# A transformer block on one core: the first token chunks prepared ahead of a branch, and a feed-forward part in 2 KB pieces

## The chip, the cores and the metric

The kernel runs on one core of a Trainium2 chip. The core has a matrix engine (TensorE, PE in the profile, with its weight loads listed as PEld), a vector engine (VectorE, DVE), a scalar engine (ScalarE, ACT), a general engine (GpSimd, POOL), and SyncE (SP), which issues the transfers between HBM and on-chip memory here. Each engine works through its own queue of instructions in order and waits on semaphores for the others. On-chip memory is SBUF (128 partitions) and PSUM, where matmuls leave their results.

The metric is device time in microseconds (us) of one execution, the median of several runs. Lower is better.

## The reference, cut to what matters

Two sequences of 1,024 tokens with 512 features go through an attention part and a feed-forward part. Each part has a layer norm ahead of it and one behind it, and adds its input.

```python
def _layernorm(x, axis=-1, eps=1e-05):
    m = jnp.mean(x, axis=axis, keepdims=True)
    v = jnp.var(x, axis=axis, keepdims=True)
    return (x - m) / jnp.sqrt(v + eps)
# attention, 32 query heads, 8 key heads, head size 128
q, k, v = hidden @ Wq, hidden @ Wk, hidden @ Wv        # each key head serves 4 query heads
gs = log_sigmoid(k) / 16
o_lin = gla_scan(softmax(q), softmax(k), v, gs)        # S = S * exp(g) + k v^T;  o = q S
y = sliding_window_attn(rope(q), rope(k), v)           # window of 64
o = bfloat16(0.5 * y + 0.5 * o_lin) @ Wo
# feed-forward, 1376 hidden features, weights rounded to NF4 in blocks of 64
h = silu(x @ dq1.T) * (x @ dq2.T)
f = h @ dq3.T
# the block
x = x + _layernorm(attention(_layernorm(x)))
x = x + _layernorm(feed_forward(_layernorm(x)))
```

## The kernel before

The 2,048 tokens are 16 chunks of 128 (NCI). A chunk is loaded, normed on DVE (bn_stats, bn_aggr, an addition, then the power of −1/2 on POOL, called `rstd`, then one subtract-and-multiply; L143 to L157), and transposed by four PE transposes into `xnT`, which holds all tokens with the features across the partitions.

The program has four stages.

**Ahead of a branch (L1162 to L1180).** All of Wk is loaded in four quarters of 512 KB (`wka`). Each is squared on ACT, its columns are summed by matmuls with ones on PE (`norms`), and DVE takes the greatest sum and compares it (`small_gates`). The flag is read by every engine and picks the fast attention (taken here) or a general one.

**Start of the fast attention (from L262).** Chunks 0 to 3 are loaded, normed (`input_norms`) and transposed (`input_transposes`; tiles `xtp`). Then the weights of key head 0 are loaded (`load_weights`: `wkv`, `wq`, `wo`), then the tables of the rotary embedding (`fcos`, `fsin`) and four constants. `part_weights` splits Wo of one head into two parts on POOL, a cast and a subtraction per query head (tile `wop`), for all four heads ahead of the first chunk (L654). Then comes the first chunk, stage by stage: `key_products` (tile `pk`), `key_softmax`, `query_products` (`pq`), whose rotary embedding (`rope`) is four POOL instructions (`qtmp`, two halves `qr`, their sum `qr`), softmaxes, and three kinds of transposes (`pt`, `tr`, `tq`).

**The attention's loop (L670 to L751).** It runs over 128 steps n, one per key head g, sequence b and chunk c of 128 tokens. Each step's order is written out by hand: `scores` (`ps`), masks on DVE, decays, exponentials on ACT, the next chunk's `query_products`, the linear part (`pa`, `ot`), `mix`, `values`, the projection of the chunk before (`project`: eight matmuls into `py`) and its sum (`collect`: `yacc`), and the next state (`pS`, `S`). The engine handles of this part are `InOrder`: what is called through them keeps the program's order on its engine, and all such instructions show the helper's line, L116. Calls through plain `nc` handles, as the norms of tokens, may be moved by the scheduler.

Two more chunks of input are normed and transposed in each of the steps n = 0 to 5:

```python
inputs = list(range(2 * CB + 2 * n, min(2 * CB + 2 * n + 2, NCI)))   # CB = 2
```

The NF4 rounding of the feed-forward weights runs inside this loop in 544 small steps on DVE and ACT, six in an even step n and three in an odd one, with its first at `BEGIN` = 6. It loads rows of weights (`xw`) and writes the rounded ones to HBM (`dq`).

**The feed-forward part (`feed_forward`, L1067).** A block is 512 tokens; there are four. `tokens` (L1104) loads a chunk of x (`xc`), norms the attention's sum (`yn`), adds, norms again (`xn`), and transposes into `x2T` (tiles `tx`). `up_weights` and `down_weights` load rounded weights (`row`, `col`) and transpose them on PE (`tw`, `tw3`) into three big tiles `w1T`, `w2T`, `w3T`. For each of 11 slices f of the hidden features, PE computes `pgate` and `pup` (L1136), ACT a sigmoid, DVE two products into `hT`. Four output chunks follow (`pf`, L1154), each normed, added and stored. The weights of slice f+2 are prepared beside slice f of the first block; the tokens of the next block are prepared at the odd f from 1 to 7. All these calls go through plain handles. The tiles lie in pools that open where the attention's pools close.

Of the kernel before, what the change touches and what calls it, by code (L numbers as in the profile page):

```python
# [1 line left out]

# [9 lines left out]
F32 = mybir.dt.float32  # L12
BF16 = mybir.dt.bfloat16
F32R = mybir.dt.float32r
# [17 lines left out]
NFT = (FF + P - 1) // P  # L32
EPS = 1e-5
# [86 lines left out]
def sandwich_kernel(ctx: ExitStack, tc: tile.TileContext, x, wq, wk, wv, wo, w1, w2, w3, out, con):  # L120
# [17 lines left out]
    yacc = keep.tile([P, NCI, HID], F32)  # L138
    dq1 = dram.tile([FF, HID], F32)
# [3 lines left out]
    def norm_stats(src):  # L143

        st = small.tile([P, 6], F32)
        nc.vector.bn_stats(st, src)
        mv = small.tile([P, 2], F32)
        nc.vector.bn_aggr(mv, st)
        ve = small.tile([P, 1], F32)
        nc.vector.tensor_scalar(ve, mv[:, 1:2], EPS, None, ALU.add)  # L150
# [4 lines left out]
    def normed(dst, src):  # L155
        mean, rstd = norm_stats(src)
        nc.vector.tensor_scalar(dst, src, mean, rstd, ALU.subtract, ALU.mult)  # L157
# [91 lines left out]
    def transposed_inputs(xtp, work, ptr):  # L249
        xnT = xtp.tile([P, KT, T], F32)  # L250
        for ci in range(NCI):
            xc = work.tile([P, HID], F32, tag="s", name=f"x{ci}")
            nc.sync.dma_start(xc, x[ci * P : (ci + 1) * P, :])
            xn = work.tile([P, HID], F32, tag="a", name=f"xn{ci}")
            normed(xn, xc)
            tp = ptr.tile([P, KT, P], F32, tag="tr", name=f"xtp{ci}")
            for kt in range(KT):
                nc.tensor.transpose(tp[:, kt, :], xn[:, kt * P : (kt + 1) * P], ident)
            nc.scalar.copy(xnT[:, :, ci * P : (ci + 1) * P], tp)
        return xnT  # L260

    def fast_attention():  # L262

        with ExitStack() as attn:
            fc = attn.enter_context(tc.tile_pool(name="fc", bufs=1))
            fs = attn.enter_context(tc.tile_pool(name="fs", bufs=4))
            xtp = attn.enter_context(tc.tile_pool(name="fxtp", bufs=1))
            wp = attn.enter_context(tc.tile_pool(name="fwp", bufs=2))
# [17 lines left out]
            xnT = xtp.tile([P, KT, T], F32)  # L286

            tokens = {}

            def input_norms(ci):  # L290

                xc = qz.tile([P, 576], F32, tag="zx", name=f"x{ci}", bufs=2)[:, :HID]
                nc.sync.dma_start(xc, x[ci * P : (ci + 1) * P, :])
                xn = qz.tile([P, 576], F32, tag=("zp", "zm")[ci % 2], name=f"xn{ci}", bufs=(2, 1)[ci % 2])[:, :HID]
                normed(xn, xc)
                tokens[ci] = xn

            def input_transposes(ci):
                xn = tokens.pop(ci)
                tp = ptr.tile([P, KT, P], F32, tag="tr", name=f"xtp{ci}")  # L300
                for kt in range(KT):
                    transpose(tp[:, kt, :], xn[:, kt * P : (kt + 1) * P])
# [909 lines left out]
```

## Time and profile before

| | us |
|---|---|
| median of 3 runs | 2175.61 (2174.6 to 2177.53) |
| the profiled execution, its own time | 2172.86 |
| its span in the trace | 2171.1 |
| PE busy in the span | 2104.6 (97%) |
| DVE busy | 1489.6 (69%) |
| ACT busy | 1362.9 (63%) |
| POOL busy | 944.1 (43%) |

The profile shows one execution. PE is the engine with the most work, and the chain of waits that ended last lies on it for 90% of the span. An average over the whole span says little about the two ends, so the view to look for is a table of busy time by stretch, in which the stages stand side by side: ahead of the branch (to 16 us), start of the attention (to 39 us), the loop (to about 1,660), the hand-over (to 1,712) and the feed-forward part. An entry in a timeline gives start and length in us, engine, line, operation, the tiles written and read (out<-in), the shape, how many instructions were put together, and in brackets how long the engine had been idle and which instruction released it. The mean granted clock of PE over the span was 0.988 of full speed.

### The profile page before, as it was taken

What the parts mean: (1) busy time and instruction counts of PE and PEld (TensorE: products, weight loads), DVE (VectorE), ACT (ScalarE), POOL (GpSimd) and SP (SyncE); (2) the same over time, 40 slices, a digit from 0 to 9 for tenths busy, and PEclk for the clock granted to TensorE, in tenths of its full rate; (3) what the DMA queues carried; (4) which work ended last, traced back from release to release, by engine and by line L of the source; (5) the groups of instructions that cost most, each with busy time, mean ns of one, the idle gap of its engine ahead of it and who ended that gap; (6) DMA issues with size and microseconds to landing.
All of it is one profiled execution on the core that took longest, in us unless ns stands there. A gap on an engine that the chain in (4) does not pass through costs nothing.

```text
span 2171.1 us, 27563 instructions
## 1 busy us (share of the span) xinstructions
PE 2104.6 (97%) x8948; PEld 1409.9 (65%) x8948; DVE 1489.6 (69%) x2822; ACT 1362.9 (63%) x3944; POOL 944.1 (43%) x1290
## 2 busy tenths in 40 slices
PE   4999999999999999999999999999996999999998
PEld 2667777777777777777777777777774544444443
DVE  3668888888788888888888888888887425142222
ACT  2568888888888888888888888888884210101000
POOL 3445555655475556456555655565452101010000
PEclk7999999999999999999999999999998999999999
DMA  5100100010010001000100100000002301000000
GB/s 194 45 15 11 59 11 15 25 49 11 9 58 10 15 15 59 11 10 20 53 11 15 39 33 11 12 11 20 13 6 68 115 27 39 0 29 0 20 0 21
DMA packets 45192, 64.52 MB, mean 30 GB/s; under 512 B 3632, under 2 KB 19632, under 8 KB 45040
## 3 DMA queue, kind: packets, MB, share of 16 engines
q1 hardware_dynamic: 45040, 62.67, 8.8%
q8 instruction: 73, 1.20, 0.2%
q14 instruction: 79, 0.65, 0.1%
HBM read 50.01 MB, written 12.65 MB: 29 GB/s over the span
## 4 chain that ended last, share of the span: by engine, by line
PE 90%; POOL 3%; ACT 2%; DVE 2%; DMA 1%; issue 1%; POOLq 0%; ACTq 0%; SPq 0%; DVEq 0%
PE pq L116 19%; PE py L116 10%; PE pk L116 10%; PE ot L116 9%; PE pgate L1136 7%; PE pf L1154 7%; PE pup L1136 7%; PE pa L116 7%; PE ps L116 5%; PE tr L116 3%; PE tq L116 3%; PE pg L116 2%; POOL qr L116 1%; PE pS L116 1%; PE pt L116 1%; ACT ps L116 1%
## 5 line engine op out<-in xcount | busy, mean ns | idle before, releaser
L116 PE MATMUL pq<-wq,xnT 128*128 128x512 f32 x1024 | 460.6, 592 | 0.0
L116 POOL TENSOR_TENSOR qtmp<-q,fcos 128x512 f32<-128x512 f32 x128 | 162.0, 1266 | 580.3 <-ACT q L116 580.3
L116 PEld LDWEIGHTS pq<-wq,xnT 128*128 128x128 f32 x1024 | 184.9, 190 | 183.7 <-issue 183.6
L116 ACT ACTIVATE zs<-xw,fbounds 128x512 bf16<-128x512 f32 (+3 forms) x416 | 287.8, 723 | 0.0
L116 PE MATMUL py<-wop,oc 128*128 128x512 f32 x1024 | 270.5, 406 | 1.3 <-ACT oc L116 1.3
L152 POOL TENSOR_TENSOR rstd<-ve,mhalf 128x1 f32<-128x1 f32 x64 | 35.7, 565 | 515.0 <-DVE ve L150 499.0
L116 ACT ACTIVATE ps<-ps,nms 128x128 f32<-128x128 f32 x512 | 175.0, 342 | 110.7 <-DVE nms L116 94.7
L116 PE MATMUL pk<-wkv,xnT 128*128 128x256 f32 x1024 | 233.4, 381 | 0.0
L116 ACT ACTIVATE pq<-pq,nmq 128x128 f32<-128x128 f32 x512 | 175.1, 342 | 91.7 <-DVE nmq L116 79.2
L1139 ACT ACTIVATE sg<-pgate 128x512 f32<-128x512 f32 (+1 forms) x44 | 26.2, 597 | 324.9 <-PE pgate L1136 324.9
L116 PEld LDWEIGHTS pk<-wkv,xnT 128*128 128x128 f32 x1024 | 195.9, 191 | 47.0 <-issue 14.1
L116 PEld LDWEIGHTS py<-wop,oc 128*128 128x128 f32 x1024 | 182.9, 189 | 36.6 <-ACT oc L116 1.7
L116 POOL TENSOR_TENSOR qr<-q,fsin 128x256 f32<-128x256 f32 x256 | 206.0, 825 | 0.0
L116 DVE SCALAR_TENSOR_TENSOR zp<-zp,zs 128x512 f32<-128x512 f32 (+3 forms) x224 | 195.4, 872 | 9.4 <-ACT zs L116 5.0
L116 POOL TENSOR_TENSOR qr<-qr,qtmp 128x512 f32<-128x512 f32 x128 | 165.8, 1295 | 9.8
L116 DVE SCALAR_TENSOR_TENSOR zm<-zm,zs 128x512 f32<-128x512 f32 (+3 forms) x192 | 163.0, 849 | 5.7 <-ACT zs L116 3.0
L1136 PE MATMUL pgate<-x2T,w1T 128*128 128x512 f32 (+1 forms) x352 | 160.4, 594 | 0.0
L1136 PE MATMUL pup<-x2T,w2T 128*128 128x512 f32 (+1 forms) x352 | 158.2, 592 | 0.0
L116 DVE TENSOR_TENSOR ps<-ps,fwin 128x512 f32<-128x512 f32 x128 | 89.2, 697 | 96.3 <-PE ps L116 95.4
L1154 PE MATMUL pf<-w3T,hT 128*128 128x512 f32 (+1 forms) x352 | 151.8, 592 | 0.0
L116 PE MATMUL ps<-kT,qrT 128*128 128x128 f32 x1024 | 136.5, 276 | 0.2
L116 DVE TENSOR_REDUCE nmq<-pq 128x4 f32<-128x512 f32 x128 | 87.8, 686 | 59.4 <-ACT q L116 59.4
(125 smaller groups left out, 4078.9 us busy)
## 6 DMA issues: line engine op xcount, KB each, us to landing
wq<-in_L_attn_Wq_dram SPq DMA_DIRECT2D x8, 1024.0 KB, 6.1
wo<-in_L_attn_Wo_dram SPq DMA_DIRECT2D x8, 1024.0 KB, 5.1
xw<-in_L_ffn_w_dram SPq DMA_DIRECT2D x20, 256.0 KB, 2.6
dq<-zp SPq DMA_DIRECT2D x20, 256.0 KB, 2.0
row<-dq SPq DMA_DIRECT2D x20, 256.0 KB, 2.8
x<-_attn_hidden_states_dram SPq DMA_DIRECT2D x16, 256.0 KB, 2.7
xc<-_attn_hidden_states_dram SPq DMA_DIRECT2D x16, 256.0 KB, 2.6
out_dram<-res SPq DMA_DIRECT2D x16, 256.0 KB, 2.0
```

The lines of the kernel that those rows point to most:

```text
L116: return lambda *args, **kwargs: self.tc.keep_in_program_order(getattr(self.engine, name)(*args, **kwargs))
L152: nc.gpsimd.tensor_tensor(rstd, ve, mhalf, ALU.pow)
L1136: nc.tensor.matmul(pg[:n, :], lhsT=wT[:, kt, f * P : f * P + n], rhs=x2T[:, kt, :], start=kt == 0, stop=kt == KT - 1)
L1139: nc.scalar.activation(sg[:n, :], ps[0][:n, :], AF.Sigmoid)
L1154: nc.tensor.matmul(pf, lhsT=hT[:n, f, m * P : (m + 1) * P], rhs=w3T[:n, f, :], start=f == 0, stop=f == NFT - 1)
```

## The change

Five things change.

1. Ahead of the branch, chunks 0 to 3 are loaded between the quarters of Wk, then the first `wkv` and `wq` and both tables. The four chunks are normed in place and transposed there, in an order written out for DVE, ACT and PE. `xnT`, the weight tiles (two sets) and the tables are now permanent tiles.
2. Chunks 4 to 15 are loaded after the branch into eight places of a tile `tokens`, which takes the second buffer of `wop`; `wo` and the small constants come after x4 and x5. A chunk's place is loaded again (12 to 15) once it was transposed.
3. `part_weights` of key head 0 is called for two heads behind the first chunk's transposes and for two inside step n = 0.
4. Two chunks of input in the steps n = 0 and 1, then one per step to n = 9. `BEGIN` is 2.
5. The feed-forward part becomes a class: 44 separate pieces of 2 KB per partition (`w1`, `w2`, `w3`, `hT`, 11 each) in place of the big tiles; buffers of tokens, rows and columns in the attention's `wqs`, `wos` and `tables`; transposed tokens written over `xnT`; and all its calls on DVE, ACT and PE through `InOrder` handles, in this order for the first block: tokens and transposes of chunks 0 to 3, row transposes of slices 0 and 1 for both weights, then the loop. The matmuls and transposes are as many as before.

```diff
+    xnT = keep.tile([P, KT, T], F32)
+    wkvs = [keep.tile([P, KT, 2 * D], F32, name=f"wkv{i}") for i in range(2)]
+    wqs = [keep.tile([P, KT, GRP * D], F32, name=f"wq{i}") for i in range(2)]
+    wos = keep.tile([P, GRP, HID], F32)
+    tables = keep.tile([P, 2, NCH, D], F32)
...
+    def chunk_transposed(xn, ci, ptr, transpose, copy):
+        tp = ptr.tile([P, KT, P], F32, tag="tr", name=f"xtp{ci}")
+        for kt in range(KT):
+            transpose(tp[:, kt, :], xn[:, kt * P : (kt + 1) * P])
+        copy(xnT[:, :, ci * P : (ci + 1) * P], tp)
...
+            staging = parts_tile("tokens").rearrange("p i h d -> p (i h) d").bitcast(F32)
+            def staged(ci):
+                return staging[:, ci % (2 * GRP), :]
             def input_norms(ci):
...
+                normed(staged(ci), staged(ci))
             def input_transposes(ci):
...
+                chunk_transposed(staged(ci), ci, ptr, transpose, nc.scalar.copy)
+                if ci + 2 * GRP < NCI:
+                    chunk_loaded(staged(ci + 2 * GRP), ci + 2 * GRP)
...
-            for ci in range(2 * CB):
-                input_norms(ci)
-                input_transposes(ci)
-            weights = {0: load_weights(0)}
+            for ci in range(AHEAD, AHEAD + 2):
+                chunk_loaded(staged(ci), ci)
...
+            weights = {0: (*first_weights, parts_tile("wop0"), load_out_weights(0))}
             qb = load_const("fbounds", [P, 16], F32, con["bounds"])
+            for ci in range(AHEAD + 2, AHEAD + 2 * GRP):
+                chunk_loaded(staged(ci), ci)
...
-            for h in range(GRP):
-                part_weights(0, h)
             key_products(0)
...
             softmax_transposes(0)
-            BEGIN = (NCI - 2 * CB) // 2
+            for h in range(2):
+                part_weights(0, h)
+            arriving = iter(range(AHEAD, NCI))
+            BEGIN = 2
             for n in range(N_):
                 g, b, c = chunks[n]
-                inputs = list(range(2 * CB + 2 * n, min(2 * CB + 2 * n + 2, NCI)))
+                inputs = list(islice(arriving, 2 if n < 2 else 1))
...
                     for ci in inputs[1:]:
                         input_norms(ci)
+                    if n == 0:
+                        for h in range(2, GRP):
+                            part_weights(0, h)
...
+        def tokens(self, ci, xc):
+            yn = self.next("yn")
+            normed(yn, yacc[:, ci, :], self.vector)
+            self.vector.tensor_tensor(yacc[:, ci, :], xc, yn, ALU.add)
+        def token_norms(self, ci):
+            xn = self.next("xn")
+            normed(xn, yacc[:, ci, :], self.vector)
+            return xn
...
+        def hidden(self, f, gate, up, sg):
+            n = min(P, FF - f * P)
+            self.vector.tensor_tensor(sg[:n, :], sg[:n, :], gate[:n, :], ALU.mult)
+            self.vector.tensor_tensor(self.hT[f][:n, :], sg[:n, :], up[:n, :], ALU.mult)
+        def run(self, f0, ready):
...
+                for f in range(f0 if tb == 0 else 0, NFT):
+                    gate = self.up_product(0, tb, f)
+                    sg = self.sigmoid(f, gate)
+                    if row:
+                        self.up_weights(0, row[0], row[1][0])
+                    if tb == 0:
+                        col = next_down(col)
+                    up = self.up_product(1, tb, f)
+                    if row:
+                        self.up_weights(1, row[0], row[1][1])
+                        row = loaded_up(next(ups, None))
+                    self.hidden(f, gate, up, sg)
...
+                    ci = (tb + 1) * self.MB + (f - 2) // 2
+                    if f >= 2 and ci < min(NCI, (tb + 2) * self.MB):
+                        if f % 2 == 0:
+                            if xn is not None:
+                                self.token_transposes(ci - 1, xn)
+                            xc = self.load_tokens(ci)
+                        else:
+                            self.tokens(ci, xc)
+                            xn = self.token_norms(ci)
...
+            F.xc, F.yn, F.xn, F.sg = ([wqs[i][:, j, :] for i in range(2)] for j in range(4))
+            F.rows = [wos[:, j, :] for j in range(4)]
...
+            for ci in range(F.MB):
+                F.tokens(ci, F.load_tokens(ci))
+                F.token_transposes(ci, F.token_norms(ci))
             for f in range(2):
-                up_weights(f)
...
+                for i in range(2):
+                    F.up_weights(i, f, F.load_up(i, f))
+            F.run(0, 2)
...
         for kt in range(KT):
             nc.sync.dma_start(wka[:, kt, :], wk[kt * P : (kt + 1) * P, :])
-            nc.scalar.activation(wka[:, kt, :], wka[:, kt, :], AF.Square)
+            if kt % 2:
+                for ci in (kt - 1, kt):
+                    chunk_loaded(chunks[ci], ci)
+        first_weights = load_weights(0)
+        load_tables("fcos", "fsin")
...
+        for ci in range(2):
+            normed(chunks[ci], chunks[ci], vector)
+        squares(0)
+        squares(1)
+        transposed(0)
+        squares(2)
+        transposed(1)
+        squares(3)
+        normed(chunks[2], chunks[2], vector)
         most = wkp.tile([1, 2], F32)
-        nc.vector.tensor_reduce(most, norms, AX.X, ALU.max)
+        vector.tensor_reduce(most, norms, AX.X, ALU.max)
...
+        normed(chunks[3], chunks[3], vector)
+        transposed(2)
+        transposed(3)
```

## The prediction

> **What bounds the kernel now.** I read the table of busy time by stretch first (stretch; its length, busy time and instructions of PE, PEld, DVE, ACT, POOL; granted clock; share of the DMA engines; GB/s).
>
> ```profile
> 0.00:16.00 16.00, 8.70 (x16) 1.44 (x16) 1.50 (x3) 5.51 (x5) 0.77 (x8) 1.00 0.35 131
> 16.00:39.00 23.00, 3.61 (x15) 2.89 (x16) 8.24 (x17) 1.75 (x3) 10.20 (x14) 0.57 0.77 243
> 85.00:114.00 29.00, 27.49 (x137) 20.09 (x136) 18.11 (x45) 17.55 (x57) 13.40 (x22) 1.00 0.12 35
> 169.00:1642.00 1473.00, 1471.03 (x7000) 1082.12 (x6998) 1224.40 (x2275) 1213.06 (x3563) 841.45 (x1117) 1.00 0.07 23
> 1660.00:1680.00 20.00, 9.17 (x37) 6.00 (x35) 10.92 (x25) 2.42 (x8) 2.33 (x4) 0.78 0.49 157
> 1680.00:1712.00 32.00, 25.75 (x92) 14.96 (x93) 22.20 (x55) 9.29 (x15) 6.27 (x11) 0.82 0.43 132
> 1712.00:2125.00 413.00, 413.00 (x1065) 188.09 (x1064) 119.44 (x225) 38.80 (x67) 15.55 (x28) 1.00 0.07 21
> ```
>
> PE is full from 169 to 1642 us and from 1712 to 2125 us. Its idle time, 66 us, lies at both ends and where the attention hands over to the feed-forward part; only there can the change win or lose, since the matmul and transpose counts stay. Next, the timeline between the branch and the first key product (start, length, engine, line, instruction, idle before it):
>
> ```profile
> 29.36 0.61 POOL L116 CAST wop<-wo 128x512 fp32r<-128x512 f32 x1 [7.13 <-DMA wo<-in_L_attn_Wo_dram]
> 30.01 0.69 DVE L146 BATCH_NORM_STATS2 st<-x 128x6 f32<-128x512 f32 x1 [7.20 <-DMA x<-_attn_hidden_states_dram]
> ...
> 33.72 0.55 POOL L152 TENSOR_TENSOR rstd<-ve,mhalf 128x1 f32<-128x1 f32 x1
> 34.24 1.26 POOL L116 TENSOR_TENSOR wop<-wo,wop 128x512 fp32r<-128x512 f32 x1
> 34.31 1.48 DVE L157 TENSOR_SCALAR xn<-x,mv,rstd 128x512 f32<-128x512 f32 x1 [2.59 <-POOL rstd L152]
> ...
> 39.30 1.06 PE L116 MATMUL pk<-wkv,xnT 128*128 128x256 f32 x2
> ```
>
> Chunk 2's tokens arrive late, then its `rstd` (a power, on POOL) waits behind the casts and subtractions of part_weights, and pk of chunk 0 starts at 39.30. The reader should also see that an `xn` beside a POOL subtraction takes 1.48 us; the two at 21.65 took 1.16 together. Last, the hand-over:
>
> ```profile
> 1668.52 0.69 DVE L116 TENSOR_TENSOR yacc<-yacc,py 128x512 f32<-128x512 f32 x1 [3.64 <-PE py L116]
> 1671.14 0.69 DVE L1110 TENSOR_TENSOR yacc<-xc,yn 128x512 f32<-128x512 f32 x1 [1.48 <-DMA xc<-_attn_hidden_states_dram]
> 1678.23 0.55 DVE L157 TENSOR_SCALAR xn<-yacc,mv,rstd 128x512 f32<-128x512 f32 x1 [0.53 <-POOL rstd L152]
> 1682.44 0.55 DVE L157 TENSOR_SCALAR xn<-yacc,mv,rstd 128x512 f32<-128x512 f32 x1 [0.59 <-POOL rstd L152]
> 1690.90 1.49 PE L1136 MATMUL pgate<-x2T,w1T 128*128 128x512 f32 x2
> ```
>
> Four token chunks come at 4.2 us each, because the scheduler put the next chunk's statistics beside this one's.
>
> **Part 1, ahead of the branch.** Removed behind it: four x loads, their norms and sixteen transposes, the loads of the first weights and tables. Added before it: the same. Squares take 1.06 us each on ACT, the norms' matmuls of one quarter about 1.75 us (16 from 5.67 to 14.37, the first slow), a group of four transposes 1.1 with its copy .58. In the new hand-written order, PE does quarter 0 until 9.07, quarter 1 until 10.8, tx0 to 11.25, quarter 2 from 13.0 (its square waits behind copy 0 on ACT), tx1, quarter 3 until 18.72. Maximum and comparison take 1.57, so the flag stands at about 20.3 instead of 15.97: +4.3. The norm of chunk 3 and its transposes end at 23.9. After the flag the branch took .7 (SP) to 1.0 (POOL). In SP's queue the x loads stand between the quarters, and weights and tables behind them: the last square started at 8.26 with 2 MB read, 1 MB of x adds 2.5 us at the quarters' pace (.5 MB in 1.26), 2.5 MB of weights and tables 7.7 at the 341 GB/s that the hand-over reached: about 18.5, so the flag and not a load sets the start. The first pk then starts at about 24.5, instead of 39.30: −14.8, give or take 1 for the waits within the two interleaved chains.
>
> **Part 2, what that gain runs into.** part_weights moves from ahead of the first chunk into it: eight POOL instructions (casts of .61, subtractions of 1.26). In the compiled order of the new kernel a cast, a subtraction and a cast stand ahead of the rope of the first queries, a subtraction inside it, four more in n=0. In the old trace (S is the start of pk) the rope's last addition ended at S+14.17; now at S+17.35. Behind POOL's queue stand the `rstd` of chunks 6, 7, 8 and 11, and DVE, in its own order, waits for each before qs(0), the mask of scores(0) and qs(1). Followed instruction by instruction with the old durations: mask(0) S+24.25 instead of S+18.15, pa(0) S+27.0 instead of S+21.4, scores of n=1 S+39.6 instead of S+30.86. That is 8.75 lost of the 14.8; I add .5 for n=1. The first of them waits for wo, now issued at about 26 behind x4, x5 and three constants; with the median landing of 5.1 it is there at 31, ahead of its turn at 33.9 (S+9.4); with the 10.1 that the first wo took here, POOL waits 2.3 more. Bounds: nothing lost, if the part_weights lie in POOL's idle time (POOL is busy 9.85 of the 18 us after 39), and 14.8, all of it. I take the followed chain, as it uses the new order. Net −5.55.
>
> **Part 3, the loop.** Inputs come one per n for n=2 to 9, formerly two for n=0 to 5. Transposes stay 1.09 per chunk, but the second of each old pair waited .67 for the ACT copy of the first (2.0 us in three for the first 100 us), and its pairs' own seam goes too: .84 for each of four n, −3.4. Bounds −3.4 and 0. The rounding steps start at n=2 instead of 6, while DVE also has the norms. One full pair of n costs DVE 19.7 to 20.7 us of 25 with rounding (stretches of 25 us from 169 on); two input norms add 2×1.6 (.69+.18+.14+.55), against a PE pair of 24.9+2×1.1=27.1. DVE keeps 3 us spare: 0. If each `rstd` waits as long as the one above (2.59), that is eaten, which is rival C. At the end no rounding stands beside the last ropes: −.35 (the slowed ones on POOL there); bounds 0 and −1.
>
> The 1.48 us norm beside POOL lost .9 against .58 for its like; if all eight norms meet a POOL operation, DVE loses 7.2 us in all. The spare time, four pairs of 3 us, covers that, so the sum stays; without cover it would be −4.65+7.2=+2.55. The Trainium skill, "SBUF — State Buffer", section "SBUF: two separate sides", has a rule for it that speaks against this change: VectorE and GpSimd arbitrate for a shared port pair by an exclusive lock, so that the later one fully blocks. The trace agrees in kind, with one .9 us loss. By the rule a norm can lose a whole POOL operation (1.27, the rope's), 8×1.27=10.2, and the sum without cover would be +5.5.
>
> **Part 4, the hand-over.** xc is loaded into memory that is free earlier, so the 1.48 wait goes. But DVE now runs the token chain strictly in order. One chunk: statistics to scaled 1.84 (2134.71 to 2136.55 in the output stage, `rstd` included), to the addition .58, to the second statistics .73, second norm 1.84, to the next .62: 5.61. The first statistics, formerly hoisted, come after the last `yacc`: 1669.12. The fourth xn starts at 1669.12+3×5.61+4.99=1690.94 instead of 1686.64: +4.30. Four row transposes instead of three precede pgate: .96 more (2.89 for three), of which I count .35, since the old ones contain waits of .2 to .5 for copies. Together +4.65; bounds +.4 (the hoisted statistics 1.84 less the xc wait 1.48, if the chunks interleave after all) and +6. PE's clock is .50 from 1675 to 1690 already, so longer gaps there cost no more.
>
> **Part 5, the rest.** SP's queue holds the same loads, earlier; x12 to x15 wait for a free slot and hold up no weights, which were issued before. From f=1 on, a token chain (5.61) and two `hidden` products (1.4) share DVE for two f (2×8 matmuls of .592, 9.5 us): 0, up to +6.4 if each of twelve chunks loses one `rstd` wait of .53. The output tail is the same chain: 0.
>
> **Sum.** −5.55−3.4−.35+4.65=−4.65. The profiled execution took 2172.86 us (span 2171.1 and 1.76 around it) and would come to 2168.2; it stands 2.75 below the median, so on the median 2175.61−4.65=2171.0. A difference under 0.2% (4.35 us) counts as none here: 2171.26 to 2179.96.
>
> **Rivals.** A, the gain is kept: POOL's added work finds its idle time. Then −14.8−3.4−.35+4.65=−13.9, 2161.7. For it: POOL is half idle in this stretch. Against: in the old trace the same casts delayed `rstd` by 2 us.
> B, the gain is eaten: the flag comes still later or the chain loses all 14.8. Then 0−3.4−.35+4.65=+.9, 2176.5: the moved work is done but doesn't shorten anything. For it: PE was busy only 1.19 of the 5 us from 48 to 53, so DVE and POOL set this chain, not pk.
> C, slower: DVE becomes the bound for n=2 to 9. Demand by pair 20.3+3.2+2×(.9 lost beside POOL+2.59 of waiting)=30.5 against PE's 27.1: 4×3.4=13.6 over the forecast, 2184.6. It decides from 1.8 us of waiting per norm. For it: 2.59 and .95 us waits at such norms. Against: a fixed order leaves waits elsewhere to absorb them; DVE at 85 to 114 was only 18.11 of 29 busy with four norms a pair.
>
> **How the numbers follow.** Forecast as summed .50, A .18, B .19, C .13. The forecast's own range is 2167 to 2175 (±1 for pk's start, ±2 for the chain, ±1.5 at the hand-over). Faster: A whole and .28 of the forecast, which lies just inside the bound: .46. Slower: C and .02 of B, .15. Same: the rest, .39. The range 2162.5 to 2180 takes in A's nearer half and leaves out C and A's far end.
>
> **What would show it.** First pk at 24 to 26; scores of n=1 about 40 us after it; single xtp groups without the .67 wait; fourth xn of the feed-forward part 22 us after the last `yacc`; no PE idle in the feed-forward loop. It is wrong if PE idles between 60 and 280 us, where rounding and norms meet, or if the token chain needs under 4.5 us per chunk.

## The result

The changed kernel took 2170.72 us (median of 13 runs, 2169.30 to 2172.95) against 2175.58 for the kernel before beside it (13 runs, 2172.54 to 2177.53). The ratio is 0.9980 (95% interval 0.9971 to 0.9988): faster by 4.9 us, just over the 0.2% that this text counts as a difference. (The ratios here are those of the record; they differ a little from the quotients of the medians, in this case 0.9978.) The forecast was 2171.0. Measured again (experiment 9) it was 2172.56 against 2175.07, ratio 0.9984 (0.9975 to 0.9993).

The profiled execution of the changed kernel spans 2170.9 us and took 2172.95, the highest of its 13 runs. The profiled one of the kernel before took 2172.86, nearly the lowest of its own. So the two traces differ by 0.1 us where the medians differ by 4.9.

Most of that goes with the granted clock, whose mean is on record for every run. The kernel before, measured beside the experiments, took 2176.8, 2174.8 and 2172.8 us where the mean clock was 0.986, 0.987 and 0.988 (medians of 27, 23 and 6 runs), and its trace has 0.988. The changed kernel took 2173.0 and 2171.0 us at 0.987 and 0.988 (5 and 9 of its 24 runs in both measurements; the others had 0.989 and 0.990), and its first trace has 0.987. So the traces compare a favourable execution of the one with an unfavourable execution of the other. At the same clock the two kernels lie 1.8 to 1.9 us apart; the rest of the 4.9 comes with the changed kernel's higher clock. A trace shows in which stage time went, but not a total to better than some 2 us.

First the busy time by stretch of the changed kernel (columns as before).

```profile
16.00:39.00 23.00, 13.30 (x43) 7.87 (x44) 9.83 (x27) 7.77 (x22) 9.24 (x17) 0.88 0.69 218
57.00:85.00 28.00, 23.64 (x110) 16.48 (x109) 15.90 (x38) 15.57 (x48) 11.02 (x18) 0.94 0.13 38
85.00:114.00 29.00, 27.10 (x125) 19.81 (x124) 21.14 (x45) 21.63 (x64) 13.66 (x20) 0.94 0.00 1
1660.00:1680.00 20.00, 5.08 (x20) 3.17 (x18) 12.01 (x28) 2.39 (x4) 2.95 (x6) 0.71 0.12 30
1680.00:1712.00 32.00, 26.59 (x93) 15.42 (x94) 8.25 (x16) 8.40 (x14) 1.45 (x3) 0.81 0.31 97
1712.00:2125.00 413.00, 413.00 (x1067) 188.06 (x1065) 136.84 (x260) 38.82 (x68) 19.78 (x36) 1.00 0.08 25
```

From 16 to 39 us PE works 13.3 us instead of 3.6: the first key product comes sooner. But from 57 to 85 and to 114 it works less than before (23.6 and 27.1 us against 26.2 and 27.5), at a clock of .94, and from 1660 to 1680 only 5.1 us instead of 9.2. From 1712 to 2125 PE is full in both kernels. Second, the timeline of the first chunk.

```profile
24.42 4.83 PE L118 MATMUL pk<-wkv,xnT 128*128 128x256 f32 x16
...
35.09 0.61 POOL L118 CAST wop<-wos 128x512 fp32r<-128x512 f32 x1 [0.72 <-DMA wos<-in_L_attn_Wo_dram]
35.78 1.26 POOL L118 TENSOR_TENSOR wop<-wos,wop 128x512 fp32r<-128x512 f32 x1
36.98 0.61 POOL L118 CAST wop<-wos 128x512 fp32r<-128x512 f32 x1
37.55 1.27 POOL L118 TENSOR_TENSOR qtmp<-q,tables 128x512 f32<-128x512 f32 x1
...
40.15 1.26 POOL L118 TENSOR_TENSOR wop<-wos,wop 128x512 fp32r<-128x512 f32 x1
41.37 1.26 POOL L118 TENSOR_TENSOR qr<-qr,qtmp 128x512 f32<-128x512 f32 x1
...
43.27 0.70 DVE L166 TENSOR_SCALAR tokens<-tokens,mv,rstd 128x512 f32<-128x512 f32 x1 [3.95 <-POOL rstd L161]
...
46.89 1.51 DVE L166 TENSOR_SCALAR tokens<-tokens,mv,rstd 128x512 f32<-128x512 f32 x1 [1.54 <-POOL rstd L161]
```

Two casts and a subtraction stand ahead of the rope (`qtmp`), a second subtraction inside it. DVE waits 3.95 and 1.54 us for two `rstd` that stand behind them. Third, the hand-over.

```profile
1664.25 0.69 DVE L118 TENSOR_TENSOR yacc<-yacc,py 128x512 f32<-128x512 f32 x1 [3.64 <-PE py L118]
...
1669.68 0.55 DVE L118 TENSOR_SCALAR wq<-yacc,mv,rstd 128x512 f32<-128x512 f32 x1 [0.67 <-POOL rstd L161]
...
1674.97 0.55 DVE L118 TENSOR_SCALAR wq<-yacc,mv,rstd 128x512 f32<-128x512 f32 x1 [0.66 <-POOL rstd L161]
...
1680.39 0.55 DVE L118 TENSOR_SCALAR wq<-yacc,mv,rstd 128x512 f32<-128x512 f32 x1 [0.73 <-POOL rstd L161]
...
1685.81 0.55 DVE L118 TENSOR_SCALAR wq<-yacc,mv,rstd 128x512 f32<-128x512 f32 x1 [0.73 <-POOL rstd L161]
...
1691.00 4.32 PE L118 MATMUL pgate<-xnT,w 128*128 128x512 f32 x8
```

These are the four second norms of the first block (their target, in the attention's `wq`, is `xn`): 5.3 to 5.4 us apart, where the kernel before needed 4.2. The fourth comes 21.6 us after the last sum, formerly 18.1. So the first gate product starts at the same time as before, 1691.0, though the attention ended 4.3 us sooner.

### The profile page after: what moved, and what is told of

Read it like the earlier page. It is cut to its first block, busy times and chain, and to the rows that moved or that the text cites. A ratio compares the mean times of both kernels' runs of the same rounds, so it can differ in the third digit from the quotient of the medians.

```text
span 2170.9 us, 27580 instructions
## 1 busy us (share of the span) xinstructions
PE 2110.2 (97%) x8948; PEld 1413.5 (65%) x8948; DVE 1492.8 (69%) x2822; ACT 1363.6 (63%) x3944; POOL 945.4 (44%) x1290
## 4 chain that ended last, share of the span: by engine, by line
PE 88%; DVE 4%; ACT 3%; POOL 3%; issue 1%; DMA 0%; POOLq 0%; ACTq 0%; DVEq 0%
PE pq L118 18%; PE py L118 10%; PE ot L118 9%; PE pk L118 9%; PE pgate L118 7%; PE pout L118 7%; PE pup L118 7%; PE pa L118 7%; PE ps L118 5%; PE tr L118 3%; PE tq L118 2%; PE pg L118 2%; POOL qr L118 1%; ACT ps L118 1%; PE pt L118 1%; PE pS L118 1%
## 5 line engine op out<-in xcount | busy, mean ns | idle before, releaser
L118 POOL TENSOR_TENSOR qtmp<-q,tables 128x512 f32<-128x512 f32 x128 | 162.5, 1270 | 586.4 <-ACT q L118 586.2
L118 ACT ACTIVATE wq<-pgate 128x512 f32<-128x512 f32 (+1 forms) x44 | 26.3, 597 | 323.9 <-PE pgate L118 323.9
L118 POOL TENSOR_TENSOR qr<-q,tables 128x256 f32<-128x256 f32 x256 | 206.4, 828 | 0.0
L118 PE MATMUL pgate<-xnT,w 128*128 128x512 f32 (+1 forms) x352 | 159.0, 594 | 0.0
L118 PE MATMUL pup<-xnT,w 128*128 128x512 f32 (+1 forms) x352 | 158.3, 592 | 0.0
L118 PE MATMUL pout<-w,hT 128*128 128x512 f32 (+1 forms) x352 | 151.8, 592 | 0.0
```

The source lines that it names most:

```text
L118: return lambda *args, **kwargs: self.tc.keep_in_program_order(getattr(self.engine, name)(*args, **kwargs))
```

## The experiments

Starts of PE instructions, worked out from the traces, in us against the kernel before (negative is earlier). "n=2", "n=4" and "n=12" are the query products of those steps (they are issued one step ahead, so that those of n=3 and n=4 bound most of step n=2), "last projection" the last `py`, "gate" the first `pgate`. "Median" is against the kernel before measured beside the same kernels.

```
                       first pk    n=2    n=4   n=12  last proj.   gate     end   median
changed                   -14.9   -4.4   -1.6   -4.5        -4.3   +0.1    -0.1     -4.9
changed, second trace     -15.2   -4.5   -1.9   -4.8        -5.1   -1.2    -2.0     -2.5
1 tokens_interleaved      -14.5   -4.3   -2.6   -4.9        -6.5   -5.2    -5.8     -6.5
2 tokens_free             -14.8   -4.8   -3.1   -5.4        +1.9  -15.4   -16.4    -19.2
3 parts_late              -15.6  -12.8   -9.5  -11.8       -11.5   -7.2    -7.7    -10.6
4 start_behind            -10.5   +0.3   +2.7   -0.1        +0.2   +4.5    +4.1     +0.9
5 begin6                  -15.3   -5.0   -6.3   -9.4        -8.1   -3.7    -4.1     -6.9
6 pairs                   -15.5   -5.4   -0.3    0.0        -1.3   +3.1    +2.5     -0.5
7 late_free               -15.2  -14.0  -10.4  -12.7        -6.6  -24.0   -24.9    -27.5
8 late_tail               -13.9  -12.4   -6.6   -9.4        -2.4  -20.0   -20.9    -24.8
10 norms_kept             -14.3  -12.5   -8.5   -1.9        -1.8   +2.5    +1.8     -1.7
11 late_free_b4           -14.8  -13.7  -13.3  -16.4        -8.5  -25.8   -26.7    -29.6
12 late_free_b6           -15.0  -14.1  -13.8  -16.8       -10.9  -28.2   -29.1    -29.9
```

### 1. The token chain interleaved by hand

```diff
-                F.tokens(ci, F.load_tokens(ci))
-                F.token_transposes(ci, F.token_norms(ci))
+                F.vector.tensor_scalar(yn, yacc[:, ci, :], *first.pop(), ALU.subtract, ALU.mult)
+                F.vector.tensor_tensor(yacc[:, ci, :], xc, yn, ALU.add)
+                stats = norm_stats(yacc[:, ci, :], F.vector)
+                if ci + 1 < F.MB:
+                    first.append(norm_stats(yacc[:, ci + 1, :], F.vector))
+                F.vector.tensor_scalar(xn, yacc[:, ci, :], *stats, ALU.subtract, ALU.mult)
+                F.token_transposes(ci, xn)
```

> The token chain of the first feed-forward block keeps a fixed order, but the statistics of the next chunk's sum stand between this chunk's second statistics and its scaling. Theory (the forecast's step: the strict order costs 5.6 us per chunk against 4.2): the fourth scaled chunk comes about 18.7 us after the last sum of the attention instead of 21.6 (1.84 for the first statistics, which stay behind it, .58, .73, 2.3, then three times 4.2), so the time falls by 2.5 to 3.5, to about 2167.7. Rival (the cold clock and the sixteen row transposes set the first gate product, not the chain): within 1 us of the changed kernel.

From the start of the last projection to the first gate product it took 25.8 us, against 28.9 in the changed kernel and 24.6 in the kernel before: 3.1 us back of the 4.4 lost, as the theory said. The fourth scaled chunk came 18.4 us after the last sum (18.7 expected). The median was 2169.43 (ratio 0.9973, 0.9963 to 0.9984): against the kernel before beside it, 1.6 us more than the changed kernel gained in its first measurement and 4.0 more than in its second, so the medians bear out the 3.1 only roughly. The strict order is the cause of these 3.1 us. The rest is put down here to the statistics of the first chunk, which stay behind the last sum; no run moves these alone.

### 2. The first tokens free to move

```diff
+            vector = nc.vector if ci < self.MB else self.vector
             yn = self.next("yn")
-            normed(yn, yacc[:, ci, :], self.vector)
-            self.vector.tensor_tensor(yacc[:, ci, :], xc, yn, ALU.add)
+            normed(yn, yacc[:, ci, :], vector)
+            vector.tensor_tensor(yacc[:, ci, :], xc, yn, ALU.add)
```

(The same choice of handle stands in `token_norms`.)

> The first block's token instructions on DVE go through plain handles; all buffers stay as in the changed kernel. In its compiled order most of them then stand inside the attention's last steps, where the strict order of the changed kernel kept them behind the last sum. Theory: only four groups of transposes with their copies (about 1.3 us each) and sixteen row transposes (3.8) remain between the last projection (2.1) and the first gate product: 11 us instead of 28.9, so about -17, 2154; a loss of up to 2 inside the attention's tail. Rival A: DVE's 15 us of token work delays the masks and sums of the last steps by as much as it saves: -5 at most. Rival B: the fixed order was not what held the tokens back (loads or buffers do): -2 at most.

2156.76 us, ratio 0.9914 (0.9901 to 0.9928): 14 us under the changed kernel. The timeline of this kernel at the hand-over:

```profile
1668.28 2.13 PE L118 MATMUL py<-wop,oc 128*128 128x512 f32 x8 [1.34 <-ACT oc L118]
1670.24 1.04 PE L118 MATMUL ptr<-ident,wq 128*128 128x128 f32 x8
...
1671.73 1.08 PE L118 MATMUL ptr<-ident,wq 128*128 128x128 f32 x8 [0.45 <-DVE wq L166]
...
1673.04 1.14 PE L118 MATMUL ptr<-ident,wos 128*128 128x128 f32 x8 [0.22 <-ACT xnT L118]
...
1674.49 1.14 PE L118 MATMUL ptr<-ident,wos 128*128 128x128 f32 x8 [0.31 <-ACT w L118]
...
1675.47 2.74 PE L118 MATMUL pgate<-xnT,w 128*128 128x512 f32 x6
```

PE goes from the last projection to the transposes without a gap, and the gate follows 7.2 us after that projection's start instead of 28.9. Each chunk of four transposes took half as long as in the changed kernel, where the clock was halved from 1668.5 to 1692.4; here it was full from 1665.5 on. 21.7 us are won here; 6.2 of them are lost again inside the attention, behind n=100 (last projection +1.9 instead of −4.3). About half of that loss lies in the last two steps: PE waited 3.8 us for DVE, which had a token's statistics in hand, and half the clock followed for 6.8 us, against a wait of 2.3 and half the clock for 3.4 at the same place of the changed kernel. Loads and buffers didn't hold the tokens back; the fixed order did. In the kernel before, the tokens' buffers lay in pools that opened when the attention's closed. In the changed one they lie in the attention's own tiles, so that the work could have started sooner, and the order that came with it forbade this.

### 3. part_weights out of the first chunk

```diff
-            for h in range(2):
-                part_weights(0, h)
...
-                    if n == 0:
-                        for h in range(2, GRP):
-                            part_weights(0, h)
...
                 state_products(n)
+                if n == 0:
+                    with tc.issue_after(keys[1]["last"].ins):
+                        for h in range(GRP):
+                            part_weights(0, h)
```

(`last` is the last POOL instruction of the second `key_softmax`.)

> All four pairs of cast and subtraction of key head 0 stand behind the second key rope on POOL, where POOL idled 8.6 us in the changed kernel. Theory (they are what delays the first chunk: 8.75 by the forecast, 10.5 in the trace of the changed kernel): scores of n=1 come 31 to 33 us after the first key product instead of 41.4, and the time falls by 7 to 10, to 2161 to 2164. Rival A: the norms of chunks 6 to 11, for whose rstd DVE waits, set this chain: scores of n=1 not before 38, time -3 at most. Rival B: the casts now delay the first projection or the next rope: gain at n=1, given back by n=4.

2165.30 us, ratio 0.9955 (0.9941 to 0.9968). The scores of n=1 came 33.7 us after the first key product instead of 41.4 (30.9 in the kernel before), a little over the range that the theory gave. At n=12 the gain over the kernel before is 11.8 instead of 4.5, the median 5.4 under the changed kernel's: less than the 7 expected, but clear. The casts are what ate most of the early start: 7.7 of the 10.5 us came back. POOL in this kernel:

```profile
34.26 1.26 POOL L118 TENSOR_TENSOR qtmp<-q,tables 128x512 f32<-128x512 f32 x1 [0.29 <-ACT q L118]
35.48 1.41 POOL L118 TENSOR_TENSOR qr<-q,tables 128x256 f32<-128x256 f32 x2
36.96 1.26 POOL L118 TENSOR_TENSOR qr<-qr,qtmp 128x512 f32<-128x512 f32 x1
...
56.44 0.61 POOL L118 CAST wop<-wos 128x512 fp32r<-128x512 f32 x1
57.13 1.28 POOL L118 TENSOR_TENSOR wop<-wos,wop 128x512 fp32r<-128x512 f32 x1
```

The rope runs unbroken and its last part starts 4.4 us sooner (36.96 instead of 41.37; 3.7 counted from the first key product), and the casts wait until 56.

### 4. The preparation behind the branch again

```diff
-            if kt % 2:
-                for ci in (kt - 1, kt):
-                    chunk_loaded(chunks[ci], ci)
-        first_weights = load_weights(0)
-        load_tables("fcos", "fsin")
...
+            for ci in range(AHEAD):
+                chunk_loaded(staged(ci), ci)
+                input_norms(ci)
+                chunk_transposed(staged(ci), ci, ptr, transpose, nc.scalar.copy)
+            first_weights = load_weights(0)
+            load_tables("fcos", "fsin")
...
+            for h in range(GRP):
+                part_weights(0, h)
             key_products(0)
```

> Undoes the part ahead of the branch alone: chunks 0 to 3, weights and tables are loaded, normed and transposed behind it, and part_weights stands ahead of the first key product, while buffers, single inputs, rounding from n=2 and the feed-forward part stay as in the changed kernel. Theory (the preparation gained a net 4.4 by n=2 in the traces): flag at 16, first key product 33 to 39, time +3 to +6, 2174 to 2177. Rival A: the gain was only better buffering of the loads, which stays: within 1.5. Rival B: with the casts out of the first chunk it is even faster: -2 to -5.

2176.85 us, ratio 1.0005 (0.9996 to 1.0014): no difference from the kernel before, and 3.4 to 5.8 over the changed one by its two measurements, as the theory said. But the first key product came at 28.8, not at 33 to 39: with eight places for tokens instead of two, and the casts behind the key products on POOL, 10.5 of the 14.9 us are won without touching the branch. They didn't help either: PE then waited 9.1 us for `kr`, a sum of the key rope that stood behind the casts on POOL, and the scores of n=1 came at 70.4, as in the kernel before (70.2). What moved ahead of the branch is worth the 4.4 us that are left at n=2 and n=12.

### 5. Rounding from n=6

```diff
-            BEGIN = 2
+            BEGIN = 6
```

> The rounding starts at n=6 as before the change, all else as changed. Theory (the forecast's 3.4 for single transposes was eaten because DVE rounds beside the norms: the changed kernel took 18.3 us from the query product of n=3 to that of n=4 where the kernel before took 15.7): these two lie under 16.5 us apart and the gain over the kernel before at n=12 rises from 4.5 to 6 to 8; time -1.5 to -3.5, unless the rounding's later end costs something at the hand-over (at most 0.5). Rival (the singles are worth nothing by themselves, the rounding is hidden): gain at n=12 within 0.5 of 4.5 to 5.4, time within 1.

At n=12 the gain is 9.4 us, more than expected; 2169.37 us, ratio 0.9972 (0.9961 to 0.9983), is 1.4 under the changed kernel, just short of the low end. The query products of n=3 and n=4 lie 14.2 us apart, against 18.3 in the changed kernel. So 4.1 of the 4.9 us between the two at n=12 lie in this one stretch, step n=2, the first with rounding; another 0.6 lie ahead of n=2, where neither kernel rounds yet. The waits of PE show it; first the changed kernel from 85 to 100 us, then the one with the rounding later, from 55 to 200 (engine and instruction, what it waited for: us, times, longest):

```profile
PE ot L118 <- DVE A L118: 0.9, 1, 0.9
PE tq L118 <- DVE qs L118: 0.8, 1, 0.8
PE xtp L118 <- ACT qrT L118: 0.2, 1, 0.2
```

```profile
PE tq L118 <- DVE qs L118: 1.7, 1, 1.7
PE tr L118 <- POOL qr L118: 1.7, 3, 1.1
PE xtp L118 <- ACT xnT L282: 1.4, 2, 0.7
```

The waits for `A`, for the copy `qrT` and one for `qs` are gone (the 1.7 that remains is the query of n=1, before the rounding in both). What made them late, in the timeline of the changed kernel:

```profile
85.16 1.27 POOL L118 TENSOR_TENSOR qtmp<-q,tables 128x512 f32<-128x512 f32 x1 [8.25 <-ACT q L118]
...
89.10 0.55 POOL L161 TENSOR_TENSOR rstd<-ve,mhalf 128x1 f32<-128x1 f32 x1
...
89.69 0.55 DVE L166 TENSOR_SCALAR tokens<-tokens,mv,rstd 128x512 f32<-128x512 f32 x1 [2.55 <-POOL rstd L161]
90.15 0.20 DVE L118 RECIPROCAL zrb<-zra 128x8 f32<-128x8 f32 x1
...
90.38 0.69 DVE L118 TENSOR_TENSOR xw<-xw,zrb 128x512 f32<-128x512 f32 x1
...
92.72 0.66 PE L118 MATMUL tq<-ident,qs 128*128 128x128 f32 x4 [0.78 <-DVE qs L118]
...
94.25 0.70 PE L118 MATMUL ot<-A,vm 128*128 128x256 f32 x2 [0.88 <-DVE A L118]
```

DVE waits 2.55 us for one `rstd`, which stands behind the rope on POOL, and then works off rounding steps (`zrb`, `xw`) before `qs` and `A`, which PE needs. In the kernel with the later rounding the compiled order is another: both `rstd` of this step stand ahead of the rope, and DVE hardly waits.

```profile
83.71 1.17 POOL L161 TENSOR_TENSOR rstd<-ve,mhalf 128x1 f32<-128x1 f32 x2 [7.45 <-DVE mv L157]
84.30 0.55 DVE L166 TENSOR_SCALAR tokens<-tokens,mv,rstd 128x512 f32<-128x512 f32 x1 [0.39 <-POOL rstd L161]
84.74 1.26 POOL L118 TENSOR_TENSOR qtmp<-q,tables 128x512 f32<-128x512 f32 x1
```

So the earlier rounding cost what it did together with the order that came with it. How much the late `rstd` costs and how much the rounding steps behind it is not shown apart.

PE idles 1.9 us in this step of the changed kernel, and its clock is halved from 95.0 to 98.4. The halving doesn't belong to the step. The kernel of experiment 1 has the same instructions in the same order on every engine up to the norms of the hand-over, and waits here as long, but its clock stayed full:

```profile
94.27 0.70 PE L118 MATMUL ot<-A,vm 128*128 128x256 f32 x2 [0.87 <-DVE A L118]
94.81 0.59 PE L118 MATMUL ot<-A,kv 128*128 128x256 f32 x2
95.24 0.38 PE L118 MATMUL pS<-kv,kh 128*128 128x128 f32 x2
96.31 0.66 PE L118 MATMUL xtp<-ident,tokens 128*128 128x128 f32 x4 [0.69 <-ACT qrT L118]
```

The last three took 0.84, 0.64 and 1.12 us in the changed kernel. From the query product of n=3 to that of n=4 it is 17.2 us here, so the halving is worth 1.0 of the 4.1 us, and waits and order about 3.

Behind the query products of n=4 the two kernels take the same time. That doesn't show rounding beside norms to be free: in the compiled order of the changed kernel the last of the twelve norms starts at 91.52 us, in step n=2, and only the transposes come one chunk per step up to n=9. Experiment 10 has norms beside the rounding for longer.

### 6. Pairs of inputs

```diff
-                inputs = list(islice(arriving, 2 if n < 2 else 1))
+                inputs = list(islice(arriving, 2 if n < 6 else 1))
```

> Two chunks of input per step for n=0 to 5 as before the change, rounding still from n=2. Theory (the forecast's step: a pair costs .67 of waiting for the copy and some seam): gain at n=12 falls by 2.7 to 3.4, time +2.5 to +3.5, 2173.5. Rival (other waits fill these steps, so the pairs' waits are hidden or replaced): gain at n=12 within 1 of that of the changed kernel.

2175.83 us, ratio 1.0000 (0.9991 to 1.0009): 5.1 over the changed kernel, and at n=12 4.5 later. Experiments 5 and 6 can be put in a square, from n=2 to n=12, with the kernel before as its fourth corner, though that one differs in more: pairs with rounding from n=6 stand for 0 (the kernel before), singles with rounding from n=6 give −4.4, pairs with rounding from n=2 give +5.4, and both together −0.1 (the changed kernel). Singles are worth 4.4 or 5.5 us, more than the forecast's 3.4, and the earlier rounding costs 4.3 or 5.4. The waits of PE from 55 to 200 us have the old pairs again:

```profile
PE xtp L118 <- ACT xnT L282: 4.5, 6, 1.1
PE tq L118 <- DVE qs L118: 2.5, 2, 1.7
PE tr L118 <- POOL qr L118: 1.6, 3, 1.0
...
```

### 7 and 8. Both losses undone, with free and with hand-placed tokens

The first is the edits of 2 and 3 together. The second puts the chain of chunk k at the end of step 123+k, instead of the free handles:

```diff
+                y = norm_stats(yacc[:, k, :], vector) if k < 4 else None
+                if k:
+                    stats = norm_stats(yacc[:, k - 1, :], vector)
+                    vector.tensor_scalar(wqs[0][:, k - 1, :], yacc[:, k - 1, :], *stats, ALU.subtract, ALU.mult)
+                if k < 4:
+                    vector.tensor_scalar(tail["yn"][k], yacc[:, k, :], *y, ALU.subtract, ALU.mult)
+                    vector.tensor_tensor(yacc[:, k, :], tail["xc"][k], tail["yn"][k], ALU.add)
```

> Both undone at once: part_weights behind the second key rope, and the first block's token instructions through plain handles. Theory (the two losses lie at different ends and add): the sum of the two single gains by their medians, 5.4 and 14.0, gives 2151; by their traces, 7.6 and 16.3, 2147. Rival (the gains overlap): over 2153.

> part_weights behind the second key rope; the first block's token chain written out by hand into the attention's last five steps, one chunk a step, after the rounding has ended, in buffers free by then; transposes after the attention as in the kernel with plain handles. That kernel lost 6.2 us within the attention's tail against the changed one. Theory (the scheduler put the tokens beside the last rounding steps and ahead of the masks): the last projection starts within 2 us of the kernel with part_weights late, and the time is 2143 to 2148. Rival (any token work in the tail delays PE by as much): like late_free, 2147 to 2152.

Free: 2148.84 us, ratio 0.9880 (0.9864 to 0.9895), between the two sums of the theory. The gains lie at different ends and add. By hand: 2151.47, ratio 0.9885 (0.9870 to 0.9901), where the rival had it. From the query product of n=126 to the last projection it took 40.2 us, against 35.7 with free tokens and 33.5 in the kernel of experiment 3, whose tail has no tokens. PE waited there for the state on DVE:

```profile
PE pa L118 <- DVE S L118: 5.7, 3, 4.1
PE pa L118 <- DVE sw L118: 1.5, 2, 1.2
...
```

Token work in the tail isn't free, wherever it was put in these two kernels.

### 9. The changed kernel again

> The changed kernel unaltered, for a second trace. Its first trace spans 2170.9, as long as that of the kernel before, though the medians are 4.9 apart. Theory (half-clock windows of 3.4 us fall at other places in each execution; the first trace had three in busy stretches, at 60.9, 95.0 and 1654.9, where the kernel before had none but at the known idle places): a second trace spans 2167 to 2170, with other places of the windows inside the busy stretches, and the gain at n=12 lies between 4.5 and 6.5. Rival (the first trace is typical and the medians mislead): span over 2170.5, median within 1 of that of the kernel before.

Its trace spans 2169.0, as the theory had it, but not for the theory's reason: the half-clock windows stand at the same places as in the first trace, at 60.4, 94.6 and 1654.5 (60.9, 95.0 and 1654.9). That the two agree is no proof that the windows belong to the kernel. The kernel of experiment 1, with the same instructions in the same order up to the hand-over, has neither the second nor the third, though PE waited as long at both places (for `S`, ahead of the third, 2.3 us in each). The kernel of experiment 2, the same up to 1490 us, doesn't have the second. So the windows differ between executions of the same instructions, as the theory said, and these two executions happened to be alike.

The two traces of the changed kernel run 0.8 us apart by the last projection, 1.3 by the gate and 2.0 by the first output product; in the second the half clock of the hand-over lasts 20.5 us and not 23.9. That the kernel before was 2.7 faster in its only trace than in its median goes with the clock too: 0.988 in the trace, and 0.986 or 0.987 in 50 of the 56 runs beside the experiments. Where the windows lay in those runs isn't on record.

### 10. Norms of the inputs kept in place

```diff
-                normed(staged(ci), staged(ci))
+                normed(staged(ci), staged(ci), vector)
```

> Changed kernel with the norms of chunks 4 to 15 kept in their written places on DVE; part_weights stays where the change put it. Theory (the first chunk loses because DVE, in its own order, waits for rstd values that stand behind the casts on POOL, as well as for the late rope): the mask of scores(0) comes 2 to 4 us earlier, the gain over the kernel before at n=2 rises from 4.4 to 6 to 8, time -2 to -4. Rival A (the late rope alone sets it): gain at n=2 within 1 of 4.4. Rival B (kept norms come too late for their transposes): slower by over 1.

At n=2 the gain was 12.5 us, more than the theory said, and at n=12 it was 1.9; 2173.40 us, ratio 0.9989 (0.9980 to 0.9998), 0.8 over the changed kernel beside it. The loss behind n=2 is rival B's: kept norms come too late for their transposes (PE waited 6.7 us for tokens and 5.3 for `A` from 55 to 210 us), though its “over 1” in the time wasn't reached. This is the one kernel in which norms really stand beside the rounding up to n=9 (the last starts at 188.7 us), and it lost 10.6 us from n=2 to n=12, 6.6 of them behind n=4. As a test of what delays the first chunk it is not clean, since with the norms gone the compiled order also put the casts behind the rope.

### 11 and 12. The best kernel with the rounding later

> The best kernel so far (part_weights late, first tokens free to move) with the rounding from n=4. Theory (two of the four steps in which rounding stood beside norms are cleared, and the rounding ends about two steps later, near the tokens' place): gain at n=12 up by 2 to 3 on that of the best kernel, of which the tail gives back up to 1; 2146 to 2148. Rival (the later end of the rounding collides with the tokens in the last steps): 2149 to 2152.

> The same with the rounding from n=6. Theory: gain at n=12 up by 4 to 5 on that of the best kernel, the tail gives back 1 to 3, since the rounding now ends in step 127: 2145 to 2148. Rival: the tail gives back all of it, 2149 to 2153.

2145.44 us (ratio 0.9856, 0.9841 to 0.9871) and 2145.14 (0.9858, 0.9843 to 0.9873). They beat the kernel before by 1.4%, and the changed kernel beside them (2172.56) by 1.25%. By their traces the gain at n=12 is 3.7 and 4.1 larger than in experiment 7. From there to the last projection that one lost 6.1 us, and these lose 7.9 and 5.9: 1.8 is given back in the first and nothing in the second (up to 1, and 1 to 3, were expected). The later end of the rounding need not be the cause of the 1.8: the first had half the clock for 6.8 us at this end and the second for 3.4, as experiment 7 had.

## Why the prediction was right, step by step

The time (2171.0, measured 2170.72) and its direction were right. The agreement to 0.3 us is luck. Two terms of the sum were off in the traces, the start by 1.1 us and the loop by 3.3, so that the traces gain 0.1 and 2.0 us and not 4.65. The sum started from the traced execution, 2172.86 us at a clock of 0.988, and at that clock the changed kernel took 2171.0, 1.9 less. The rest of the 4.9 by which the medians differ comes with a higher clock, which the sum didn't have as a term.

**Start.** "The first pk then starts at about 24.5": 24.42, and 24.11 in the second trace. The flag stood at 21.10 (20.3 in the forecast).

**What the gain runs into.** The forecast lost 9.25 of 14.8 by n=2; the traces lost 10.5 and 10.7. Step by step from the first key product: the rope's end 18.2 (17.35), mask 25.0 (24.25), pa 28.0 (27.0), scores of n=1 41.4 (39.6). The first three are late by about 1, the last by 1.8, of which the forecast had added 0.5. The first delay fits `wo`, which landed when the casts were due and not before: POOL waited 0.72 us for it. The mechanism was right, and experiment 3 shows it, with 7.3 us at n=12. A rival (A, all the gain kept) fell with it.

**The loop.** This is the term that failed: −3.4 for single inputs and 0 for the earlier rounding, where from n=2 to n=12 nothing was won (−0.1 and −0.3 in the traces). The singles give −4.4 to −5.5 and the earlier rounding costs 4.3 to 5.4 (experiments 5 and 6). So the step that failed is “DVE keeps 3 us spare: 0”, which compared averages by pair. It also took the norms to come one per step from n=2 to 9, as they are written; the compiled order had them done in n=2. There one late `rstd` ahead of rounding steps was enough, with a wait of 2.55 us, nearly the 2.59 of rival C. The forecast's own sign of being wrong, PE idle between 60 and 280 us where rounding and norms meet, was there: 1.9 us in n=2. C had the mechanism, and was wrong for this kernel to charge it in four pairs of steps. Where the norms stand as written (experiment 10), the loop lost 10.6 us, near C's 13.6 less 3.4; that it lost them by C's terms isn't shown.

**The norms beside POOL.** The norm at 46.89 took 1.51 us beside a subtraction on POOL that ended at 48.11, and .55 is usual. The Trainium skill ("SBUF — State Buffer", "SBUF: two separate sides") says that a port pair shared by VectorE and GpSimd goes to the operation that needs it first, for the whole of the instruction, while the other is blocked, and this row fits that. (So do three norms of 1.48 us in the kernel before, at 34.31, 36.80 and 49.38, of which the forecast counted one.) The forecast had spare time on DVE take such losses. This norm had none: it stood ahead of the first mask (49.42) in DVE's order, so that its loss belongs to the start. None of the four norms behind 59 us took more than .55.

**The hand-over.** +4.65 in the forecast, +4.4 and +3.9 in the two traces, from 5.4 us per chunk instead of the 5.61 of the output stage. Experiment 1 gives 3.1 of it back with the order alone. What the forecast didn't see was how much more lay there: that the new buffers allow the whole chain to move under the attention (experiment 2).

**The rest.** PE waited for nothing from 1720 us on. The gains that the runs show behind the gate product, 0.2 and 0.9 us, lie between it and the first output product, where the half clock ends.

**Rival B** (the gain eaten, 2176.5) was close by the first trace and not by the medians.

## What to carry to other kernels

An early start is worth what the next chain leaves of it: follow the queue of each engine past the moved work, and look for what was moved into it (here eight POOL instructions ate half of 14.9 us). Spare time on average is no cover in the order that an engine really runs; one wait ahead of optional work is enough. Look up that order before pricing it, since the place where a call is written need not be the place where it runs. Where buffers are rearranged so that work could start sooner, see that no pinned order keeps it where it was. And compare the granted clocks before two traces are compared.

## What the runs showed of the hardware

The recorded clock has steps of 3.41 us, and a step needn't be idle to be followed by half the clock: in the changed kernel steps with PE busy for 26%, 32% and 52% (worked out from the matmul records) were, and one with 62% wasn't; in the kernel of experiment 1, steps with 57 and 59% weren't. The share alone doesn't settle it: one step with about half in the kernel before wasn't either, and one with 55% in the kernel of experiment 8 was. The Trainium skill ("TensorE: Matmul & The Clock Gate", "Part 1: The HAM clock gate") tells of idle windows of this length. In this kernel an idle time of 1.65 us within one (0.78 and 0.88, ahead of 95.0) was enough.

Whether a wait is followed by half the clock can differ between executions of the same instructions: the waits of step n=2 were in both traces of the changed kernel and not in those of experiments 1 and 2, where the step took 17.2 us instead of 18.1 to 18.3. The length of the half clock at the hand-over differed by one step of 3.41 us between two executions of the same kernel.
